# A two-layer graph network: layer 1's attention weights carry both exponentials, its fetched rows go to the matmul as they are, and TensorE counts the used columns

## The chip, the cores and the metric

One core of one Trainium2 chip runs the whole program. The metric is the device time of one execution in microseconds (us); lower is better. Engines are called PE (TensorE), DVE (VectorE), ACT (ScalarE), POOL (GpSimd) and SP (SyncE, which only issues DMAs here).

## The reference, cut to what matters

There are 16 graphs of N = 1024 nodes with F = 256 features. Layer 0 is a graph attention with batch normalisation; the change leaves its code alone. Layer 1 has H = 4 heads and is where the change lies:

```
fts = inputs @ Wh                      # inputs: layer 0's result after residual and layernorm
f1, f2 = fts @ w1h + b1h, fts @ w2h + b2h
coefs_logits = softmax(leaky_relu(f1[:, None] + f2[None, :], 0.2) - 1e9 * (1 - adj))
coefs = ah * coefs_logits + (1 - ah) * softmax(adj)
vals = coefs @ fts + bh
head = elu(vals + inputs)              # mean of the four heads, residual, layernorm
```

The adjacency is sparse: an edge from i to j has a probability that falls with both indices. In a block of 128 target rows, most columns have no edge at all. The kernel therefore finds, for each block of rows, the columns that are used, fetches only these columns' rows of the table, and sums over them.

## The kernel before, in words

N is cut into K = 8 blocks of P = 128 rows. For block q at most CAPS[q] × 128 used columns are fetched, with CAPS = (6, 4, 3, 3, 3, 3, 2, 2): 26 fetches of 128 columns per graph, numbered c. For each c there is `xc[c]`, 128 rows of a table `xe_dram` (256 features, a one, four values of a first exponential and four of a second), and `mc[c]`, the same columns' 128 mask values for the block's rows (bf16). `A[it]` holds an exponential of f1 for the rows of block `it`, for four heads, spread over all partitions.

The softmax of a leaky ReLU is split so that no exponential is taken per edge. For head h the weight of an edge is max(A, exp(-0.8 f2)) times the mask, made by DVE (`Unit.weights`, L1356, one 128x128 operation per column block and head, 1664 in all). The other factor, exp(f2), is multiplied into the fetched row by ACT (`Unit.values`, L1347, 128x257, also 1664). PE multiplies the two (`gather`, L1378) and gets the sum over edges and, in column 257, the divisor.

Work is laid out in **units**: one unit is one block of rows and two heads (`hp`), 16 units per graph, 256 in all. Nothing here is left to a scheduler: the body stands in `tc.manual_schedule()`, and each engine works its instructions in the order in which the loop issues them. One pass n of the loop handles six units at different stages: `add` (n-3, DVE), `turned` (n-2, ACT), `addends` (n, POOL), `gather` (n, PE), `linear` (n-2, PE), `mix` (n-1, DVE) and `turn` (n-1, PE), weights and values for n+2, `exps` (n-3, ACT), `share` (n, ACT), `sum` (n-3, DVE), `close` (n-4). Every second unit has the heavy `sum`, which ends with layernorm statistics and, on POOL, a power of -0.5 (`inv_std`, L159).

After this each pass issues the **side steps** of the next graph, by a table from pass number to steps (`side`): load of h, mask and x, `elu`, `used` (which columns have an edge), `places` (prefix counts by matmul), `pick` (eight one-hot tiles `oh` by DVE, L1134, with matmuls that turn them into index lists), `residual` (transpose of h by PE, then add and layernorm statistics by DVE), `norm`, `factors`, `spread`, `scale`, `table`, `split`, `total`, `neighbours` (the sum over all neighbours by PE, then one addition by DVE, L1293) and the fetches. A graph's fetches begin in pass 11 of the graph ahead of it.

PSUM tiles of the side steps come from one pool of two buffers, `ps_s`. Three queues issue DMAs: SP (loads, stores and the transposed mask load L1061), POOL (indirect fetches and `mask`, L1278, which turns a block of the mask into fp32), and ACT (layer 0 alone).

In these terms `used` works on the transposed mask in SBUF, `mt`: it takes a maximum over the 128 rows of each block by halving (L1082, L1087) and one reduction (L1091).

Of the kernel before, what the change touches and what calls it, by code (L numbers as in the profile page):

```python
# [8 lines left out]
F32 = mybir.dt.float32  # L9
# [10 lines left out]
P = 128  # L20
# [7 lines left out]
def kernel(  # L28
# [93 lines left out]
    iota16 = cpool.tile([P, P], FP16, name="iota16")  # L122
# [6 lines left out]
    with tc.tile_pool(name="ipool", bufs=1) as ipool:  # L129
        ii = ipool.tile([P, P], I32, name="ii")  # L130
        nc.gpsimd.iota(ii, pattern=[[1, P]], base=0, channel_multiplier=0)
# [905 lines left out]
    with ExitStack() as l1:  # L1037
# [8 lines left out]
        class Graph:  # L1046


            def __init__(self, b):
                self.b = b  # L1050
                self.S, self.mr, self.xc, self.mc, self.A = {}, {}, {}, {}, {}

            def load_h(self):
                b = self.b
                self.h = hpool.tile([P, C, N], F32, tag="h", name=f"h_{b}")
                nc.sync.dma_start(self.h, h_dram[b])
                if b in ready1:
                    self.mt = ready1[b]
                else:
                    self.mt = m1pool.tile([P, K, N], BF16, tag="mt", name=f"mt1_{b}")  # L1060
                    nc.sync.dma_start_transpose(self.mt, adj16[b])  # L1061
                self.mv = pk.tile([P, K, 2], F32, tag="mv", name=f"mv_{b}", bufs=2)
# [7 lines left out]

            def used(self):

                b = self.b
                nc.sync.dma_start(
                    mt_dram[b % 2][0:N, :].rearrange("(k p) i -> p k i", p=P), self.mt
                )
                self.act = pk.tile([P, K, K], BF16, tag="act", name=f"act_{b}", bufs=2)
                for half in range(2):
                    ks = slice(half * K // 2, (half + 1) * K // 2)
                    view = self.mt[:, ks, :].rearrange("p k (q i) -> p k q i", i=P)  # L1080
                    t = pk.tile([P, K // 2, K, P // 2], BF16, tag="hm", name=f"un_{b}_{half}", bufs=1)
                    nc.vector.tensor_tensor(  # L1082
                        t, view[:, :, :, 0 : P // 2], view[:, :, :, P // 2 : P], ALU.max
                    )
                    n = P // 4
                    while n >= 8:
                        nc.vector.tensor_tensor(  # L1087
                            t[:, :, :, 0:n], t[:, :, :, 0:n], t[:, :, :, n : 2 * n], ALU.max
                        )
                        n //= 2  # L1090
                    nc.vector.tensor_reduce(self.act[:, ks, :], t[:, :, :, 0 : 2 * n], AX.X, ALU.max)  # L1091

            def places(self):


                b = self.b
                pp = ps_s.tile([P, K + 1, K], F32, tag="s", name=f"pp_{b}")
                for k in range(K + 1):
# [5 lines left out]
                    if k < K:  # L1104
                        nc.tensor.matmul(pp[:, k, :], tri16, self.act[:, k, :], start=(k == 0), stop=False)
                        nc.tensor.matmul(pp[:, k, :], far16, self.act[:, k, :], start=False, stop=True)
                pos = pk.tile([P, K + 1, K], F32, tag="pos", name=f"pos_{b}", bufs=1)
                nc.scalar.copy(pos, pp)
# [5 lines left out]
                nc.vector.tensor_copy(self.r16, pi)  # L1114
                nc.vector.tensor_tensor(pos[:, 0:K, :], pos[:, 0:K, :], self.r16, ALU.subtract)
# [6 lines left out]
                self.t16 = pk.tile([P, K, K * n], FP16, tag="t16", name=f"t16_{b}", bufs=2)  # L1122
# [3 lines left out]
                )  # L1126

            def pick(self, q):

                b = self.b  # L1130
                if q == 0:
                    self.pl = ps_s.tile([P, NC], F32, tag="s", name=f"pl_{b}")
                oh = pk.tile([P, K, P], FP16, tag="oh", name=f"oh_{b}_{q}", bufs=2)
                nc.vector.tensor_tensor(  # L1134
                    oh, iota16.unsqueeze(1).to_broadcast([P, K, P]),
                    self.r16[:, :, q : q + 1].to_broadcast([P, K, P]), ALU.is_equal,
                )
                n = max(CAPS)
                for k in range(K):
                    nc.tensor.matmul(  # L1140
                        self.pl[:, CAT[q] : CAT[q] + CAPS[q]],
                        oh[:, k, :], self.t16[:, k, q * n : q * n + CAPS[q]],
                        start=(k == 0), stop=(k == K - 1),
                    )
# [9 lines left out]
            def fetch_rows(self, c):  # L1154

                self.xc[c] = pk.tile([P, XW], F32, tag="xc", name=f"xc_{self.b}_{c}", bufs=14)
# [5 lines left out]
            def fetch_mask(self, c):  # L1162

                self.mc[c] = pk.tile([P, P], BF16, tag="mc", name=f"mc_{self.b}_{c}", bufs=14)
# [6 lines left out]
            def rows(self, it):  # L1171
# [3 lines left out]
                    self.A[it], a_dram[self.b][:, it * P : (it + 1) * P].partition_broadcast(P)  # L1175
                )
# [13 lines left out]
            def residual(self, k):  # L1190
                nm = f"{self.b}_{k}"
                pz = ps_s.tile([P, F], F32, tag="s", name=f"pz_{nm}")
                for oc in range(C):
                    nc.tensor.transpose(
                        pz[:, oc * P : (oc + 1) * P], self.h[:, oc, k * P : (k + 1) * P], ident
                    )
                xk = self.x[:, k, 0:F]
# [432 lines left out]
```

## Time and profile before

| | |
|---|---|
| time, median of 3 runs | 3520.68 us (3514.99 to 3521.13) |
| the profiled execution: its own time | 3522.07 us |
| its span in the profile | 3520.3 us |
| granted TensorE clock, mean | 0.859 |
| busy: PE, DVE, ACT, POOL | 77%, 80%, 55%, 43% of the span |
| layer 0, up to about | 798 us |
| layer 1, first graph's preparation, up to the first weights | 883 us |
| layer 1, one graph in the steady part (first `o` to first `o`) | 168.2 us |

The page cuts the span into 40 slices of 88 us, a digit for the busy tenths of each engine. In its list of costly groups a row gives the source line, engine and operation, output and inputs, shape and count, then busy time in all and the mean duration of one, then the engine's idle time just before these instructions and what ended most of it. Durations of neighbouring instructions on one engine overlap, so the distance from start to start is the price where an engine works without a break.

### The profile page before, as it was taken

The numbers are of one execution on the slowest core, as the hardware profiler recorded it, in microseconds if no ns is written. First come the engines' busy times: TensorE is split into PE (matmuls) and PEld (weight loads), VectorE is DVE, ScalarE is ACT, GpSimd is POOL, SyncE is SP. The second block draws the span as 40 slices with busy tenths as digits, with TensorE's granted clock in tenths as the row PEclk, the third lists the DMA queues.
The fourth block names the chain that finished last, engine by engine and source line by source line (L and its number), as shares of the span: only waits on it lengthen the run. The fifth ranks groups of instructions, "written<-read, shape, count | busy, mean of one in ns | idle before, by whom it ended". The sixth has DMA issues, their size and how long they took to land.

```text
span 3520.3 us, 44899 instructions
## 1 busy us (share of the span) xinstructions
PE 2722.9 (77%) x14567; PEld 2126.6 (60%) x14567; DVE 2804.3 (80%) x6644; ACT 1919.1 (55%) x3892; POOL 1510.7 (43%) x1425
## 2 busy tenths in 40 slices
PE   7936999994786877777777768686868686867796
PEld 6723444443675756566665657575757575756575
DVE  3369999974888787888878787878787878787888
ACT  1247777751564655555555555555556464645565
POOL 0000000003564646455646465555646464646463
PEclk9957999996897978788888888888889797978898
DMA  9796985555464747464646455554546464737441
GB/s 279 220 260 151 234 212 154 152 154 116 99 125 99 136 102 139 90 142 80 143 91 145 86 133 102 127 104 115 108 113 124 105 124 97 141 92 147 90 89 40
DMA packets 630643, 462.90 MB, mean 131 GB/s; under 512 B 286424, under 2 KB 567040, under 8 KB 624256
## 3 DMA queue, kind: packets, MB, share of 16 engines
q1 hardware_dynamic: 446016, 286.63, 30.3%
q0 software_dynamic: 183168, 170.81, 28.5%
q8 instruction: 118, 1.93, 0.2%
q10 hardware_dynamic: 1216, 2.51, 0.2%
q14 instruction: 125, 1.02, 0.1%
HBM read 257.53 MB, written 135.21 MB: 112 GB/s over the span
## 4 chain that ended last, share of the span: by engine, by line
DVE 37%; PE 26%; issue 16%; DMA 9%; ACT 6%; POOL 5%; SPq 0%; DVEq 0%; ACTq 0%; POOLq 0%
DVE w L1356 8%; PE pu L1378 7%; DMA mt<-adj 6%; PE pm L1288 4%; PE pa L584 4%; PE pw L301 4%; PE pv L1418 3%; DVE s L1398 3%; DVE v L1425 2%; DVE oh L1134 2%; DVE xs L1257 2%; POOL xc L1157 2%; PE pf L1208 2%; ACT x L1224 2%; DVE z L1396 2%
## 5 line engine op out<-in xcount | busy, mean ns | idle before, releaser
L1378 PE MATMUL pu<-g,w 128*128 128x257 f32 x3328 | 944.2, 444 | 3.1 <-ACT g L1347 3.1
L1378 PEld LDWEIGHTS pu<-g,w 128*128 128x128 f32 x3328 | 740.3, 230 | 128.9 <-ACT g L1347 3.6
L1347 ACT ACTIVATE g<-xc 128x257 f32<-128x257 f32 x1664 | 723.0, 502 | 65.5 <-DMA xc<-xe_dram,ix 55.2
L1418 PE MATMUL pv<-W1s,sT 128*128 128x256 f32 x2048 | 524.8, 402 | 269.9 <-DVE z L1394 257.2
L1418 PEld LDWEIGHTS pv<-W1s,sT 128*128 128x128 f32 x2048 | 400.3, 200 | 371.5 <-issue 267.1
L1356 DVE SCALAR_TENSOR_TENSOR w<-A,xc,mc 128x128 f32<-128x128 f32 x1664 | 586.1, 420 | 37.9 <-DMA xc<-xe_dram,ix 30.7
L1157 POOL DMA_INDIRECT xc<-xe_dram,ix x416 | 480.9, 1156 | 144.0 <-issue 121.0
L1165 POOL DMA_INDIRECT mc<-mt_dram,im x416 | 443.6, 1066 | 130.0 <-issue 110.3
L584 PE MATMUL pa<-em,wh 128*128 128x512 f32 x1024 | 451.8, 599 | 17.9 <-issue 13.4
L159 POOL TENSOR_TENSOR ors<-ors,mhalf 128x1 f32<-128x1 f32 x128 | 98.0, 766 | 788.3 <-DVE ors L158 674.1
L1429 ACT ACTIVATE m<-v,neg 128x512 f32<-128x512 f32 x256 | 183.3, 716 | 443.7 <-DVE z L1394 242.7
L1288 PE MATMUL pm<-xs,mr 128*128 128x256 f32 (+1 forms) x2048 | 292.4, 302 | 75.1 <-DMA mr<-mt 75.1
L584 PEld LDWEIGHTS pa<-em,wh 128*128 128x128 f32 x1024 | 193.7, 192 | 251.0 <-issue 236.3
L1288 PEld LDWEIGHTS pm<-xs,mr 128*128 128x128 f32 x2048 | 274.5, 206 | 78.1 <-issue 78.1
L1366 POOL TENSOR_TENSOR v<-x,bias 128x512 f32<-128x512 f32 x256 | 311.9, 1218 | 22.7 <-DVE acc L1436 13.5
L1398 DVE SCALAR_TENSOR_TENSOR s<-pu,z,s 128x256 f32<-128x256 f32 x512 | 224.3, 480 | 24.5 <-ACT s L1388 0.5
L1388 ACT ACTIVATE s<-S,q 128x256 f32<-128x256 f32 x512 | 228.9, 495 | 0.0
L1412 ACT COPY sT<-pt 128x512 f32<-128x512 f32 x256 | 148.1, 578 | 94.1 <-PE pt L1406 86.2
L540 ACT ACTIVATE e<-eb,c,s 128x1024 f32<-128x1024 f32 x128 | 155.0, 1236 | 79.1 <-DVE sm L554 42.7
L1457 ACT ACTIVATE o<-o,ors 128x256 f32<-128x256 f32 x128 | 76.8, 600 | 204.8 <-DVE ors L1454 196.3
L1293 DVE SCALAR_TENSOR_TENSOR S<-pm,X 128x256 f32<-128x256 f32 x128 | 54.0, 423 | 158.3 <-PE pm L1288 138.5
L1425 DVE TENSOR_TENSOR v<-pv,v 128x512 f32<-128x512 f32 x256 | 173.6, 678 | 0.5 <-PE pv L1418 0.5
(256 smaller groups left out, 3921.9 us busy)
## 6 DMA issues: line engine op xcount, KB each, us to landing
mr<-mt POOLq DMA_DIRECT2D x128, 512.0 KB
x<-in_x_dram SPq DMA_DIRECT2D x32, 1024.0 KB
adj<-in_adj_dram POOLq DMA_DIRECT2D x16, 2048.0 KB
mt_dram<-mt SPq DMA_DIRECT2D x16, 2048.0 KB
A<-a_dram SPq DMA_DIRECT2D x128, 256.0 KB
xe_dram<-x SPq DMA_DIRECT2D x16, 1060.0 KB
wh_dram<-wx SPq DMA_DIRECT2D x16, 1024.0 KB
wh<-wh_dram SPq DMA_DIRECT2D x16, 1024.0 KB
```

What stands on the lines that cost most here:

```text
L584: nc.tensor.matmul(acc[b, hf, oc], wh[b][:, k, oc * P : (oc + 1) * P], ems[b, k][:, hf * HALF : (hf + 1) * HALF], start=(k == 0), stop=(k ...
L1157: nc.gpsimd.indirect_dma_start(out=self.xc[c], out_offset=None, in_=xe_dram[self.b % 2], in_offset=bass.IndirectOffsetOnAxis(ap=self.ix[:, ...
L1165: nc.gpsimd.indirect_dma_start(out=self.mc[c], out_offset=None, in_=mt_dram[self.b % 2].rearrange("n (q i) -> (n q) i", i=P), in_offset=ba ...
L1288: nc.tensor.matmul(pm[:, 0:n], lhsT, self.xs[:, k, part, 0:n], start=(k == 0 and part == 0), stop=(k == K - 1 and part == 0),)
L1347: nc.scalar.mul(v, g.xc[c][:, 0:F1], g.xc[c][:, F1 + H + h : F1 + H + h + 1])
L1356: nc.vector.scalar_tensor_tensor(w, g.A[self.it][:, h, :], g.xc[c][:, F1 + h : F1 + h + 1], g.mc[c], ALU.max, ALU.mult,)
L1366: nc.gpsimd.tensor_tensor(self.v2, self.g.x[:, self.it, 0:F].unsqueeze(1).to_broadcast([P, HP, F]), bias1[:, h : h + HP, :], ALU.add,)
L1378: nc.tensor.matmul(self.pu[:, hh, 0:F1], self.w[hh][t], self.v[hh][t], start=(t == 0), stop=(t == n - 1),)
L1388: nc.scalar.mul(self.s[:, hh], g.S[it], g.q[:, it, h0 + hh : h0 + hh + 1])
L1398: nc.vector.scalar_tensor_tensor(s[:, hh], self.pu[:, hh, 0:F], z[:, hh : hh + 1], s[:, hh], ALU.mult, ALU.add)
L1418: nc.tensor.matmul(self.pv[:, hh, :], self.sT[:, hh, fc, :], W1s[:, fc, self.hp * HP + hh, :], start=(fc == 0), stop=(fc == C - 1),)
L1425: nc.vector.tensor_tensor(self.v2, self.pv, self.v2, ALU.add)
```

## The change

**Weights.** The table's exponentials become exp(f2) and exp(0.2 f2). With A = exp(0.8 f1) the weight max(A · exp(f2), exp(0.2 f2)) is the softmax's numerator up to a factor of the row. It is made per column block c for four heads: four `tensor_scalar` (multiply, maximum, both with a pointer operand) and one product with the mask over 128x512. ACT's scaled copies of the rows fall away: `gather` takes `xc[c]` as the moving side. A column block's weights serve both units of a block.

**Used columns.** A graph's adjacency rows are loaded once more, untransposed, as `rw` (2 MB, bf16). PE counts each block's edges per column by 64 matmuls with one column of ones; DVE takes the minimum with 1. The one-hot tile `oh` lies in `rw`'s buffer and has the block index innermost, so that every operand has unit steps.

**Residual.** One `tensor_tensor_reduce` adds and sums the row; the square sums are ACT's (`means`, eight Square activations with accumulator), in place of bn_stats and bn_aggr.

**Order.** A side step's matmuls and its DVE part are issued apart: `first` goes ahead of `mix` and `turn`, `after` to the end of the pass. The power of -0.5 of `sum` is issued a pass later (`power`), `close` at n-5. Weights are made three passes ahead, fetches start one pass earlier; mask and `rw` are loaded in pass 14 of the graph two ahead. Buffers: xc and mc 17 (14), w 12 of four heads, m 1, s 2.

```diff
-    iota16 = cpool.tile([P, P], FP16, name="iota16")
+    iota16 = cpool.tile([P, P, K], FP16, name="iota16")
...
+            def load_mask(self):
...
+                self.rw = pk.tile([P, K, N], BF16, tag="rw", name=f"rw_{b}", bufs=1)
+                nc.sync.dma_start(self.rw, adj16[b].rearrange("(q p) j -> p q j", p=P))
...
+            def counts(self):
+                self.pc = ps_s.tile([P, K, K], F32, tag="s", name=f"pc_{self.b}")
+                for k in range(K):
+                    for q in range(K):
+                        nc.tensor.matmul(
+                            self.pc[:, k, q : q + 1], self.rw[:, q, k * P : (k + 1) * P],
+                            ones16[:, 0:1], start=True, stop=True,
+                        )
             def used(self):
-                for half in range(2):
-                    ...
-                    nc.vector.tensor_reduce(self.act[:, ks, :], t[:, :, :, 0 : 2 * n], AX.X, ALU.max)
+                nc.vector.tensor_scalar(self.act, self.pc, 1.0, None, ALU.min)
...
+            def mark(self, q):
                 nc.vector.tensor_tensor(
-                    oh, iota16.unsqueeze(1).to_broadcast([P, K, P]),
-                    self.r16[:, :, q : q + 1].to_broadcast([P, K, P]), ALU.is_equal,
+                    self.oh[:, q], iota16, self.r16[:, q, :].unsqueeze(1).to_broadcast([P, P, K]),
+                    ALU.is_equal,
                 )
...
+            def weights(self, c):
+                it = max(q for q in range(K) if CAT[q] <= c)
+                w = self.w[c] = pk.tile([P, H, P], F32, tag="w", name=f"w_{self.b}_{c}", bufs=12)
+                xc = self.xc[c]
+                for h in range(H):
+                    nc.vector.tensor_scalar(
+                        w[:, h, :], self.A[it][:, h, :], xc[:, F1 + h : F1 + h + 1],
+                        xc[:, F1 + H + h : F1 + H + h + 1], ALU.mult, ALU.max,
+                    )
+                nc.vector.tensor_tensor(
+                    w, w, self.mc[c].unsqueeze(1).to_broadcast([P, H, P]), ALU.mult
+                )
...
             def residual(self, k):
-                nc.vector.tensor_tensor(xk, pz, xk, ALU.add)
-                nc.vector.bn_stats(st, xk)
-                nc.vector.bn_aggr(self.mv[:, k, :], st)
+                nc.vector.tensor_tensor_reduce(
+                    out=xk, in0=self.pz[k], in1=xk, scale=1.0, scalar=0.0,
+                    op0=ALU.add, op1=ALU.add, accum_out=self.mv[:, 0, k : k + 1],
+                )
...
+            def means(self):
+                nc.vector.tensor_scalar(self.mv[:, 0], self.mv[:, 0], -1.0 / F, None, ALU.mult)
+                for k in range(K):
+                    d = pk.tile([P, F], BF16, tag="d", name=f"d_{self.b}_{k}", bufs=2)
+                    nc.scalar.activation(
+                        d, self.x[:, k, 0:F], AF.Square, bias=self.mv[:, 0, k : k + 1], scale=1.0,
+                        accum_out=self.mv[:, 1, k : k + 1],
+                    )
...
-            def values(self, hh):
-                    ...
-                    nc.scalar.mul(v, g.xc[c][:, 0:F1], g.xc[c][:, F1 + H + h : F1 + H + h + 1])
-            def weights(self, hh):
-                    ...
-                    nc.vector.scalar_tensor_tensor(
-                        w, g.A[self.it][:, h, :], g.xc[c][:, F1 + h : F1 + h + 1], g.mc[c],
-                        ALU.max, ALU.mult,
-                    )
...
                     nc.tensor.matmul(
-                        self.pu[:, hh, 0:F1], self.w[hh][t], self.v[hh][t],
+                        self.pu[:, hh, 0:F1], g.w[c][:, h, :], g.xc[c][:, 0:F1],
...
+            after[-2] += [g.load_mask]
+            after[-1] += [g.load_h]
+            first[2] += [g.counts]
+            after[2] += [g.used, each(g.elu, 0)]
+            first[3] += [g.places]
+            after[3] += [g.load_x, g.placed, each(g.elu, 1)]
+            for k in range(K):
+                first[4 + k // 2] += [each(g.turn, k)]
+                after[4 + k // 2] += [each(g.residual, k)]
+            after[5] += [g.store_mask]
+            for q in range(K):
+                after[4 + q // 3] += [each(g.mark, q)]
+            after[7] += [g.means, g.norm]
+            first[8] += [g.pick, g.shares1]
+            after[8] += [g.indices, g.factors]
+            ...
+            for it, n in enumerate((11, 12, 12, 13, 13, 14, 14, 15)):
+                first[n] += [each(g.neighbours, it)]
+                after[n] += [each(g.summed, it)]
+            for it, n in enumerate((6, 7, 8, 11, 12, 12, 13, 13)):
+                after[n] += [each(g.mask, it)]
...
+            for n in range(len(units) + 6):
+                b, i = divmod(n, NU)
+                do(n - 3, "add")
+                do(n - 2, "turned")
+                do(n - 4, "power")
+                do(n, "addends")
+                if n < len(units):
+                    units[n].gather(0)
+                    units[n].gather(1)
+                do(n - 2, "linear")
+                stand(0, b, i)
+                do(n - 1, "mix", "turn")
+                for s, at in ((b + 1, i), (b, NU + i)):
+                    if s < B:
+                        made(graphs[s], at)
+                do(n - 3, "exps")
+                do(n, "share")
+                do(n - 3, "sum")
+                do(n - 5, "close")
+                stand(1, b, i)
```

`stand(0, …)` issues a pass's `first` steps and `stand(1, …)` its `after` steps, for the graph one ahead, for the one two ahead and for the graph at hand.

## The prediction

> **What bounds the kernel now.** The profile page comes first: engine totals, then the slices.
>
> ```profile
> PE 2722.9 (77%) x14567; PEld 2126.6 (60%) x14567; DVE 2804.3 (80%) x6644; ACT 1919.1 (55%) x3892; POOL 1510.7 (43%) x1425
> ...
> DVE  3369999974888787888878787878787878787888
> ```
>
> No engine is full. From slice 10 on (about 880 us) the picture repeats sixteen times: layer 1, one graph of 16 units at a time, while the side steps of the next graph are worked in. The first `o` of each graph comes 168.2 us after the one before (mean of 14 periods in the trace). To see where a period goes I cut one (graph 5) at each `v<-pv` of L1425, the first DVE step of a loop pass, and asked for busy times by stretch. Passes i = 0, 1, 4, 7, 11 and 14:
>
> ```profile
> core 0: us, PE busy (x) PEld busy (x) DVE busy (x) ACT busy (x) POOL busy (x), PEclk, DMA share, GB/s
> 1715.46:1724.31 8.85, 8.85 (x43) 7.30 (x41) 8.46 (x24) 7.77 (x18) 3.20 (x3) 1.00 0.62 168
> 1724.31:1743.08 18.77, 5.89 (x29) 4.87 (x28) 15.17 (x28) 7.77 (x14) 9.48 (x9) 0.82 1.09 267
> ...
> 1762.85:1775.77 12.92, 8.77 (x65) 7.18 (x66) 12.07 (x27) 4.51 (x10) 6.56 (x5) 0.76 0.25 76
> ...
> 1797.90:1806.37 8.47, 7.76 (x52) 7.22 (x50) 5.03 (x20) 3.32 (x7) 4.02 (x4) 0.89 0.36 62
> ...
> 1836.92:1845.53 8.61, 8.61 (x58) 8.03 (x57) 5.53 (x15) 4.42 (x11) 5.31 (x6) 1.00 0.66 111
> ...
> 1860.94:1874.38 13.44, 10.87 (x59) 9.65 (x57) 11.11 (x34) 8.52 (x22) 11.39 (x12) 0.87 0.69 111
> ```
>
> A pass lasts about as long as the busier of PE and DVE in it, and then some: summed over the 16 passes (mean of 13 graphs) the larger of the two is 152 us, the period 168. The other 16 us are waits, and the query of waits (1200 to 3200 us, 12 graphs) names them (us in total, times, longest):
>
> ```profile
> DVE S L1293 <- PE pm L1288: 88.5, 62, 3.5
> DVE h L1188 <- ACT h L1185: 36.9, 12, 3.1
> DVE x L1198 <- PE pz L1194: 27.6, 11, 3.2
> ...
> DVE f L1232 <- PE pf L1208: 23.6, 12, 2.6
> ...
> PE pv L1418 <- DVE z L1394: 207.8, 67, 15.5
> PE pl L1140 <- DVE oh L1134: 104.1, 96, 3.0
> ```
>
> A side step's matmuls stand on PE behind `turn`, so behind DVE's `mix`; DVE then waits for them at once. Two queues take turns where both have work. The period is DVE work, PE work in some passes, and this ping-pong. ACT (91.7 us a period) has slack.
>
> [...] nine L446 `tensor_scalar` of 1024 take 6.05 us (662 ns apart), while `oh`, 16 bit but with a step-0 inner operand, takes 1135 ns for 1024 and `un`, 2048 bf16, 1225. [...] of 847 `w` that run beside a POOL DMA_INDIRECT alone 3 exceed 400 ns, of 116 that meet a POOL TENSOR_TENSOR 93 do (up to 2119). [...] 16 small `r` casts, 195 ns each. [...] Here `pu` matmuls stand 217 or 425 ns apart, nothing between.
>
> ```profile
> 1700.50 1.93 DVE L1356 SCALAR_TENSOR_TENSOR w<-A,xc,mc 128x128 f32<-128x128 f32 x7 [0.89 <-DMA xc<-xe_dram,ix]
> 809.20 9.16 DVE L1134 TENSOR_TENSOR oh<-iota,r 128x1024 f16<-128x1024 f16 x8
> L1347 ACT ACTIVATE g<-xc 128x257 f32<-128x257 f32 x1664 | 723.0, 502 | 65.5 <-DMA xc<-xe_dram,ix 55.2
> L1356 DVE SCALAR_TENSOR_TENSOR w<-A,xc,mc 128x128 f32<-128x128 f32 x1664 | 586.1, 420 | 37.9 <-DMA xc<-xe_dram,ix 30.7
> ```
>
> Durations overlap, so I price by start to start: `w` 262 ns (7 in 1.93 us).
>
> **Part by part, us per graph (one period).** DVE:
> - Weights: 104 `w` at 0.262 = 27.2 go. In come 104 `tensor_scalar` of 128 with pointers: [...] 0.196, 20.4 in all; and 26 products of 128x512: 0.60 (spacing of L1436) + 0.08 behind their own last input (L1439 stands 0.12 further off) = 17.7. **+10.9**. [...]
> - `used`: L1082, L1087, L1091 (2.5 + 2.8 + 0.8) become one small operation: **-6.0**.
> - `oh`: 8 × 1.135 = 9.1 becomes 8 × 0.60 with unit steps: **-4.3** (0 if not).
> - Residual: add, bn_stats, bn_aggr (3.2 + 3.4 + 0.8) become 8 adds with an accumulator, 0.35 + 0.08 (L189 shows 346 apart with its read): 3.4 or so: **-4.0**.
> - Small new ones: +0.3. DVE total **-3**.
>
> ACT: 104 `g` (42.8) go, 8 Square with accumulator come: 128x256 is about 0.5, read 0.19 (L606): 5.5. **-37**, hidden but where DVE waits for ACT. PE: `gather` has the same shapes; +64 one-column matmuls at 26 ns (`pl` is 27) = **+1.7**; `pick` reads weights with a step of 8 elements, which no row shows: 0 to 64 × 0.1 = 6, I take 0. POOL: same operations; 8 `pow` are one pass later, so fetches no longer queue behind a `pow` that waits for DVE. Fetches and weights start a pass earlier. SP: 2 MB `rw` more per graph, behind the transpose that holds SP 14.6 us; four passes of cover (38 us), DMA share is about 0.55. If that cover goes, `counts` and PE behind it wait.
>
> Order is the large part: side matmuls now stand ahead of `mix`, their DVE halves at the end of the pass. The S, x and f waits and `pl`'s go (7.4 + 2.3 + 2.0 on DVE, 8.7 on PE). New: in pass 7 `means` sends 8 Squares to ACT and `norm`, next on DVE, waits for them: 5.5, then POOL's `pow` 1.7 and latencies: **+7.5** against 1.8 now; behind it on DVE stands the next `add`, for which PE's `linear` waits. `elu` keeps its ACT wait once (2.9).
>
> What is late next at `neighbours` is the mask: masks 4 to 6 are issued in the pass before their use, and PE waits 4.0 a period for such DMAs today (47.8 over 12).
>
> Passes rebuilt: DVE = 5.2 (even i: heavy `sum`) or 2.75 (odd) + 1.4 per column made (2, 2, 1, 2, 1, 2, 1, 2, 1, 1, 1, 1, 1, 3, 3, 2) + side: `elu` 1.4 in passes 2 and 3, `placed` 2.1 in 3, residuals and marks 2.7, 2.7, 2.1 in 4 to 6, `norm` 1.3, `factors` 1.6, `split` 1.7 and 1.6, `summed` 0.4 to 0.8, `shares` 1.2. PE = gather (per column and pass four `pu`, 0.24 each) + `linear` and `turn` 2.35 + side (`counts` 1.7; `pl` and `pf` 5.3 in pass 8; `pX` and `pm` 3.7 in 11, then `pm` 1.9 each), clock about 0.9. Larger of the two plus the waits named and some POOL blocking, i = 0 to 15: 8.3, 8, 11.5, 9.6, 9.9, 8.8, 9.2, 14.3, 10.5, 7.5, 8.7, 9, 8, 8.4, 10.8, 7.7 = 150. Pass 1 falls most (18.8 to 8: `elu` and `used` leave it), pass 7 grows. Of the kernel before, a rebuild by busy times missed 16; here most waits are counted, and I add 4: **154**, so -14 × 15 graphs = **-210**.
>
> The start: graph 0's `rw` and the h and x loads behind it must wait for layer 0's memory, issued near 799; 2 MB at the 200 GB/s of neighbouring slices is 10 us, where `used` took 7: +5. The fetches: 20 (mask and row of two blocks) at 1.25 stand ahead of mask 3, where 13 stood: +9. **+15** (5 to 20). End: close is a pass later, ACT lighter: -2 to +2, 0. Sum: 3522.07 (the profiled execution; span 3520.3 plus 1.8; 1.4 above the median) - 210 + 15 = 3327, less 1.4: **3325**.
>
> **Rivals.**
> 1. Passes overlap more than the larger-of-two rule: DVE 125 + POOL blocking 8 + pass 7's and other waits 10 = 143: 3520 - 25 × 15 + 15 = **3160**. For: PE's gather may run a pass ahead. Against: passes before never beat their busier engine.
> 2. It doesn't do what it says: [...] +11.2 × 15 = 168: **3493**. [...]
> 3. Slower: [...] (0.96 us, L1157's median): 26 × 0.96 = 25 a period, +375: **3700**. It decides from (3520 - 3325)/15/26 = 0.50 us a column. For: POOL prepares DMAs over a third of the time. Against: the casts above, and a preparation can stretch instead (up to 4.3 us beside `oh`), which costs only fetch slack.
>
> **How the numbers follow.** Likeliest case 0.52 (own range 3250 to 3400), rival 1 0.20, rival 2 and kin (waits left over) 0.15, rival 3 0.11, no change 0.02. Faster by over 0.2% (about what a measurement can tell) 0.87, within 0.02, slower 0.11. The range leaves out rival 3 and the low half of rival 1: 3170 to 3490.
>
> **What would show it.** After: period near 154; `w` products and `tensor_scalar` near 200 ns apart; `oh` 0.6; pass 1 about 8 us, pass 7 about 14 with DVE waiting for ACT's Square; no S <- pm or pl <- oh. Wrong if `tensor_scalar` lasts over 0.6 us beside POOL, or PE waits for `rw`.

## The result: 3602.93 us, slower by 2.4%

| | before | after |
|---|---|---|
| median, same chip (4 runs each) | 3517.84 us | 3602.93 us |
| ratio, 95% interval | | 1.0243 (1.0225 to 1.0261) |
| span of the profiled execution | 3520.3 us | 3601.0 us |
| first `o` of graph 0 | 940.2 us | 962.2 us |
| steady part: mean of the 16 passes' sum, 13 graphs | 168.2 us | 172.1 us |

The 81 us of span are: start +22, fourteen periods +54 (+3.9 each), the step from graph 14 to 15 +10.8, the last graph -8.2, the end +1.9. The prediction had -14 a period and +15 at the start.

Engine totals and DVE's slices of the page after:

```profile
PE 2810.2 (78%) x15591; PEld 2233.4 (62%) x15591; DVE 2777.1 (77%) x6820; ACT 1319.3 (37%) x2484; POOL 1392.6 (39%) x1425
...
DVE  4369999953877878787878787868787877878788
```

ACT lost 600 us of work and DVE 27, PE gained 87; only PE is fuller, by one percent of the span, and the program is slower. So the time has to be looked for in single passes. These are the same graph's passes i = 0, 1, 4, 7, 8, 9, 11, 14, cut at the same DVE step as before (columns as there: length, busy time of PE, weight loads, DVE, ACT, POOL, then the granted clock):

```profile
core 0: us, PE busy (x) PEld busy (x) DVE busy (x) ACT busy (x) POOL busy (x), PEclk, DMA share, GB/s
1754.25:1762.90 8.65, 8.65 (x44) 7.60 (x43) 8.27 (x25) 1.52 (x3) 3.00 (x4) 1.00 1.12 261
1762.90:1775.13 12.23, 7.86 (x39) 6.56 (x37) 6.84 (x19) 3.08 (x6) 3.74 (x4) 0.95 0.66 240
1796.76:1807.13 10.37, 7.13 (x28) 5.67 (x28) 10.03 (x27) 2.59 (x5) 4.76 (x5) 0.84 0.28 89
1826.05:1839.52 13.47, 5.44 (x28) 4.55 (x28) 7.27 (x27) 6.03 (x20) 1.78 (x2) 0.84 0.07 16
1839.52:1855.43 15.91, 15.08 (x108) 14.23 (x109) 9.25 (x25) 2.12 (x4) 10.76 (x11) 0.50 0.67 107
1855.43:1866.79 11.36, 9.79 (x39) 7.62 (x37) 6.54 (x20) 8.27 (x21) 2.22 (x2) 0.83 0.39 110
1876.87:1886.43 9.56, 8.74 (x45) 8.02 (x46) 4.69 (x15) 1.79 (x4) 0.08 (x1) 0.67 0.20 22
1906.84:1919.56 12.72, 8.00 (x52) 7.24 (x52) 12.23 (x33) 2.71 (x7) 9.46 (x10) 1.00 0.75 122
```

The eye should stop at three lines. Pass 1 lasts 12.2 us with no engine over 7.9: a wait. Pass 8 lasts 15.9 with PE at 15.1 and a clock of 0.50. Pass 9 lasts 11.4 with PE 9.8 and ACT 8.3, neither full: two engines taking turns. Against the prediction, as means over 13 graphs:

| pass | 0 | 1 | 2 | 3 | 4 | 5 | 6 | 7 | 8 | 9 | 10 | 11 | 12 | 13 | 14 | 15 |
|---|---|---|---|---|---|---|---|---|---|---|---|---|---|---|---|---|
| before | 8.8 | 19.7 | 9.9 | 9.9 | 12.9 | 11.1 | 10.7 | 9.9 | 11.3 | 9.4 | 9.8 | 8.6 | 6.7 | 7.6 | 14.8 | 7.2 |
| predicted | 8.3 | 8 | 11.5 | 9.6 | 9.9 | 8.8 | 9.2 | 14.3 | 10.5 | 7.5 | 8.7 | 9 | 8 | 8.4 | 10.8 | 7.7 |
| after | 8.7 | 11.0 | 11.6 | 10.0 | 10.4 | 9.1 | 9.8 | 13.5 | 15.9 | 11.4 | 10.1 | 9.2 | 9.8 | 10.0 | 12.9 | 8.8 |

Passes 8, 9 and 1 make 12 of the 22 us above the predicted 150; passes 10 and 12 to 15 make 8. The query of waits (same window of 2000 us, total us, times, longest) names what stands in the first three:

```profile
PE pv L1429 <- DVE z L1405: 333.1, 92, 8.0
...
DVE acc L1447 <- ACT m L1440: 92.3, 22, 4.8
...
ACT X L1308 <- PE pX L1303: 85.1, 11, 8.5
DVE f L1264 <- PE pf L1231: 66.8, 11, 6.1
...
DVE w L1192 <- DMA A<-a_dram: 47.3, 12, 5.1
DVE mv L1249 <- ACT d L1241: 45.2, 11, 4.1
```

The old waits for `pz` and `pl` are gone, as predicted, and of 88.5 us for `pm` 3.9 are left (24.5 more at the same addition, in pass 12, are listed with the releaser `remote`). In their place DVE waits for ACT's exponentials (passes 9 and 11), for `pf` (pass 8), for A (pass 1) and for the Squares (pass 7). Passes 7 and 8 as the timeline has them (start, duration, and in brackets the idle time before with its releaser):

```profile
1837.29 0.17 DVE L1249 TENSOR_SCALAR mv<-mv 128x8 f32<-128x8 f32 x1 [4.11 <-ACT d L1241]
...
1837.74 1.66 POOL L159 TENSOR_TENSOR rs<-rs,mhalf 128x8 f32<-128x8 f32 x1 [12.76 <-DVE rs L158]
...
1839.43 0.17 DVE L1251 TENSOR_TENSOR rs<-mv,rs 128x8 f32<-128x8 f32 x1 [1.77 <-POOL rs L159]
...
1840.35 3.75 PE L1429 MATMUL pv<-W1s,sT 128*128 128x256 f32 x8 [8.03 <-DVE z L1405]
...
1843.89 3.99 PE L1143 MATMUL pl<-t,oh 128*128 128x6 f16 x64
...
1847.74 6.98 PE L1231 MATMUL pf<-WW,h 128*128 128x8 f32 x32
...
1854.76 0.22 DVE L1264 TENSOR_TENSOR f<-pf,xw 128x64 f32<-128x64 f32 x1 [6.09 <-PE pf L1231]
```

DVE stands 4.1 + 1.8 us in `norm`, as forecast. PE therefore stands 8 us, and then works 15 us at a granted clock of 0.50: `pv` 426 ns apart in place of 216, `pf` 213 in place of 112. And `pl` lasts 3.99 us for 64, 60 ns each, where before it was 27.

The weights, and `oh`, at full speed (timeline; the last figure is the count in the group, its time the whole group's):

```profile
815.26 4.90 DVE L1132 TENSOR_TENSOR oh<-iota,r 128x1024 f16<-128x1024 f16 x8
...
1211.73 1.12 DVE L1192 TENSOR_SCALAR w<-A,xc 128x128 f32<-128x128 f32 x4
1212.89 0.69 DVE L1196 TENSOR_TENSOR w<-w,mc 128x512 f32<-128x512 f32 x1
```

`oh` came out as priced: 8 in 4.90 us, 602 ns apart. The product too: 609. A `tensor_scalar` is 256 ns from the next, not 196. In the steady part (13 graphs, cut as above) DVE is busy 50.6 us a graph with weights, against 36.2 before.

### The profile page after: what moved, and what is told of

Same layout as the page of the kernel before. It is cut to its first block, busy times and chain, and to the rows that moved or that the text cites. A ratio compares the mean times of both kernels' runs of the same rounds, so it can differ in the third digit from the quotient of the medians.

```text
span 3601.0 us, 45794 instructions
## 1 busy us (share of the span) xinstructions
PE 2810.2 (78%) x15591; PEld 2233.4 (62%) x15591; DVE 2777.1 (77%) x6820; ACT 1319.3 (37%) x2484; POOL 1392.6 (39%) x1425
## 4 chain that ended last, share of the span: by engine, by line
DVE 32%; PE 12%; issue 9%; DMA 9%; POOL 6%; ACT 6%; SPq 2%; another core or an unknown queue 1%; DVEq 0%; POOLq 0%; ACTq 0%
DVE w L1192 8%; PE pv L1429 4%; DMA A<-a_dram 4%; DVE w L1196 3%; PE pf L1231 3%; DVE v L1436 3%; DMA mc<-mt_dram,im 2%; DVE s L1409 2%; DVE xs L1293 2%; POOL v L1376 2%; ACT d L1241 2%; POOL mc L1173 2%; PE pl L1143 2%; DVE v L1449 2%; DMA mr<-mt 2%
## 5 line engine op out<-in xcount | busy, mean ns | idle before, releaser
L1429 PE MATMUL pv<-W1s,sT 128*128 128x256 f32 x2048 | 659.2, 479 | 566.9 <-DVE z L1405 432.8
L1429 PEld LDWEIGHTS pv<-W1s,sT 128*128 128x128 f32 x2048 | 469.1, 238 | 716.7 <-issue 478.5
L1389 PE MATMUL pu<-xc,w 128*128 128x257 f32 x3328 | 821.2, 400 | 11.3 <-DVE w L1196 9.1
L1389 PEld LDWEIGHTS pu<-xc,w 128*128 128x128 f32 x3328 | 656.6, 204 | 104.9 <-DVE w L1196 12.2
L1192 DVE TENSOR_SCALAR w<-A,xc 128x128 f32<-128x128 f32 x1664 | 508.3, 376 | 54.0 <-DMA A<-a_dram 54.0
L1165 POOL DMA_INDIRECT xc<-xe_dram,ix x416 | 417.9, 1005 | 144.0 <-issue 123.8
L1173 POOL DMA_INDIRECT mc<-mt_dram,im x416 | 426.0, 1024 | 104.9 <-issue 100.1
L1196 DVE TENSOR_TENSOR w<-w,mc 128x512 f32<-128x512 f32 x416 | 317.0, 762 | 14.2
L1463 POOL TENSOR_TENSOR ors<-ors,mhalf 128x1 f32<-128x1 f32 x128 | 72.8, 569 | 300.3 <-DVE ors L1469 284.6
L1314 POOL DMA_DIRECT2D mr<-mt x128 | 121.0, 947 | 166.2 <-PE pm L1324 139.7
L1447 DVE SCALAR_TENSOR_TENSOR acc<-m,v 128x512 f32<-128x512 f32 x128 | 87.8, 686 | 125.9 <-ACT m L1440 125.9
```

The costliest lines, as they stand in the source:

```text
L1165: nc.gpsimd.indirect_dma_start(out=self.xc[c], out_offset=None, in_=xe_dram[self.b % 2], in_offset=bass.IndirectOffsetOnAxis(ap=self.ix[:, ...
L1173: nc.gpsimd.indirect_dma_start(out=self.mc[c], out_offset=None, in_=mt_dram[self.b % 2].rearrange("n (q i) -> (n q) i", i=P), in_offset=ba ...
L1192: nc.vector.tensor_scalar(w[:, h, :], self.A[it][:, h, :], xc[:, F1 + h : F1 + h + 1], xc[:, F1 + H + h : F1 + H + h + 1], ALU.mult, ALU.max,)
L1196: nc.vector.tensor_tensor(w, w, self.mc[c].unsqueeze(1).to_broadcast([P, H, P]), ALU.mult)
L1389: nc.tensor.matmul(self.pu[:, hh, 0:F1], g.w[c][:, h, :], g.xc[c][:, 0:F1], start=(c == cs[0]), stop=(c == cs[-1]),)
L1429: nc.tensor.matmul(self.pv[:, hh, :], self.sT[:, hh, fc, :], W1s[:, fc, self.hp * HP + hh, :], start=(fc == 0), stop=(fc == C - 1),)
```

## Experiments

Two theories stood at first. **A**: the weights took work from ACT, which had slack, and gave it to DVE, the busiest engine before the change. **B**: the new order brought new waits, and these hold the period whatever DVE does. Every time below is a ratio to the kernel before on the same chip, beside the sum of the 16 passes.

### The weights alone, and everything but the weights

`b_weights` is the kernel before with this part only, its buffers included (in short):

```diff
-    weights: 4 x scalar_tensor_tensor(max, mult) per column; values: ACT, xc times exp(f2)
+    weights: 4 x tensor_scalar(mult, max) and one 128x512 product per column, shared by two units
-    nc.tensor.matmul(self.pu[:, hh, 0:F1], self.w[hh][t], self.v[hh][t], ...)
+    nc.tensor.matmul(self.pu[:, hh, 0:F1], g.w[c][:, h, :], g.xc[c][:, 0:F1], ...)
```

> The kernel before with the weights part alone: four tensor_scalar and one product of 128x512 per column block, shared by both units of a block, ACT's scaled rows gone, gather takes the fetched rows; everything else (order, used columns, one-hot tiles, residual) as before; xc and mc 17 buffers, w 12. DVE gains about 15 us a graph, ACT loses 43. Theory A: slower than the kernel before, 168 -> 176 to 184 a graph, ratio 1.04 to 1.08, more than the whole change costs, so that the rest of the change is worth -5 to -12 a graph. Rival B (the loss comes from the new order and its waits, the weights are about neutral because passes were held by waits and ACT's relief pays back): ratio 0.98 to 1.01.

`a_split` is the changed kernel with this part's arithmetic undone:

```diff
-    nc.vector.tensor_scalar(w[:, h, :], A, xc[F1 + h], xc[F1 + H + h], ALU.mult, ALU.max)   # 4 heads
-    nc.vector.tensor_tensor(w, w, mc, ALU.mult)
+    nc.vector.scalar_tensor_tensor(w[:, h, :], A, xc[F1 + h], mc, ALU.max, ALU.mult)       # 4 heads
...
+    nc.scalar.mul(w[:, h, :], w[:, h, :], xc[F1 + H + h])                                   # after exps
```

> The changed kernel with the weights alone put back to the old arithmetic: per column block and head one DVE operation (maximum with exp(-0.8 f2), then times the mask), and ACT multiplies exp(f2) into the weight (128x128, in place, after exps). Order, counts, residual and buffers stay as changed. DVE loses 104 x 0.256 + 26 x 0.61 - 104 x 0.262 = 15 us a graph, ACT gains 104 x 0.3 to 0.4 = 31 to 42. Theory A (the weights moved work from an ACT with slack onto DVE, which bounds most passes): the passes with DVE on top shorten, about -0.6 a column, 172 -> 157 to 162 a graph, total 3350 to 3440, ratio to the kernel before 0.95 to 0.98. Rival B (the period is held by the waits of passes 1, 7, 8 and 9 and by the order, whatever DVE does): 169 to 174 a graph, ratio 1.01 to 1.03. Rival C (ACT with 90 us a graph delays exps and sT): slower than the changed kernel.

| order, counts, residual | old weights | new weights |
|---|---|---|
| as before | 1 (168.2) | 1.0497, 1.0470 to 1.0523 (178.0) |
| as changed | 0.9804, 0.9776 to 0.9832 (163.3) | 1.0243, 1.0225 to 1.0261 (172.1) |

Theory A holds for the weights part as a whole, in both orders; that DVE's time is the reason is shown by `a_ts512` below, where ACT is untouched. The new weights cost 9.8 us a graph in the old order and 8.8 in the new; everything else in the change gains 5 to 6. DVE's line of the two pages says how:

```profile
PE 2779.7 (75%) x14567; PEld 2146.8 (58%) x14567; DVE 3111.0 (84%) x7060; ACT 1259.4 (34%) x2228; POOL 1455.2 (39%) x1425
```

```profile
PE 2760.2 (80%) x15591; PEld 2188.7 (63%) x15591; DVE 2479.9 (72%) x6404; ACT 1819.5 (53%) x4148; POOL 1451.1 (42%) x1425
```

The first is `b_weights`, the second `a_split`. With the weights alone DVE is busy 156.2 us a graph in place of 137.1 (+19.1), and 9.8 of it reach the period; with them undone it is busy 116.9 in place of 135.4 (-18.5), and 8.8 do. About half of a DVE microsecond reaches the end. `a_split`'s ACT multiplies a 128x128 weight and not a 128x257 row, so this cell of the table is not the old scheme to the letter. Rival C, that a busy ACT would delay `exps` and lose the gain, fell.

### What a tensor_scalar costs

`a_tsmix` gives the operations of the four heads different operands. Where an operand is a column of `xc` (a pointer), each partition has its own value; where it is a number, all have the same:

```diff
+    tensor_scalar(w[:, 0], A[:, 0], e1[0:1], e2[0:1], mult, max)
+    tensor_scalar(w[:, 1], A[:, 1], e1[1:2], 0.0,     mult, max)
+    tensor_scalar(w[:, 2], A[:, 2], 1.0,     0.0,     mult, max)
+    tensor_scalar(w[:, 3], A[:, 3], e1[3:4], e2[3:4], mult, max)
```

> The changed kernel with four different tensor_scalar of 128x128 per column block: head 0 with two pointer operands, head 1 with a pointer and an immediate, head 2 with two immediates, head 3 with two pointers (heads 1 and 2 leave their own factors out). It prices the operation. 341 ns at 128 and 540 at 512 wide are 0.52 ns an element[...]; yet two stand 256 ns apart[...]. Theory (each pointer operand has its own fixed cost): 256, about 226, about 196 ns to the next. Rival (256 ns is the fixed cost of any 128-wide tensor_scalar behind another): all three near 256.

One column block of `a_tsmix` in the timeline:

```profile
1867.13 0.34 DVE L1192 TENSOR_SCALAR w<-A,xc 128x128 f32<-128x128 f32 x1
1867.38 0.28 DVE L1193 TENSOR_SCALAR w<-A,xc 128x128 f32<-128x128 f32 x1
1867.58 0.22 DVE L1194 TENSOR_SCALAR w<-A 128x128 f32<-128x128 f32 x1
1867.71 0.34 DVE L1195 TENSOR_SCALAR w<-A,xc 128x128 f32<-128x128 f32 x1
```

Read the differences of the starts: two pointers 0.25, one 0.20, none 0.13. Over all 416 blocks the medians are 254, 196 and 135 ns: **each pointer operand costs 60 ns**, in spacing and in duration (341, 282, 222). At the 0.52 ns an element of the next run, 128 elements are 67 of the 135 ns, and 68 are left as fixed, an estimate from these two runs. The old `w`, with one pointer, fits the same sum at 1.04 ns an element (worked out below): 133, 68 and 60 are 261, measured 262. The kernel took 3562.63 us in a single run, with 169.6 us a graph: 2.5 of the 4.7 us that DVE saves (26 times 60 and 120 ns).

`a_ts512` makes one instruction of the four, and leaves out the own factors of heads 1 to 3:

```diff
-    for h in range(H): nc.vector.tensor_scalar(w[:, h, :], self.A[it][:, h, :], ...)
+    nc.vector.tensor_scalar(w, self.A[it], xc[:, F1 : F1 + 1], xc[:, F1 + H : F1 + H + 1], ...)
```

> The changed kernel with one tensor_scalar of 128x512 per column block, with head 0's two pointers, in place of four of 128x128: the other heads' own factors are left out. ACT, PE, POOL, order and DMAs are untouched. At the 256 ns of a 128-wide one, the wide one tells the slope: [...] DVE loses 104 x 0.256 - 26 x (0.40 to 0.66) = 9.5 to 16 us a graph. Theory A (DVE bounds most passes): the period falls by 60 to 90% of that, 172 -> 158 to 166, ratio 0.96 to 0.995. Rival B (waits hold it): under 3 us a graph, ratio 1.01 to 1.02.

540 ns at 512 wide against 341 at 128 is 0.52 ns an element, half of the 1.04 that an fp32 `scalar_tensor_tensor` takes in the kernel before (687 ns at 512, 1218 at 1024). So by the element a `tensor_scalar` with two pointers **is** the faster of the two. (The 574 ns to the next instruction includes the product's wait for its own input.) Ratio 0.9913 (0.9884 to 0.9942), 164.7 a graph: DVE lost 14.4, the period 7.4. Again about half, with ACT, PE and all DMAs untouched. That is the cleanest evidence for theory A; of the expected 60 to 90% only 51 came, because the wait for A grew from 47 to 82 us in the window and ate a part.

### The waits one by one

**A of block 2.** On SP's queue this load stands behind the next graph's transposed mask load, issued in pass 14 (11.0 us of SP in one such pass).

```diff
-    after[NU - 5 + 2 * it] += [each(g.rows, it)]
+    after[NU - 5 + 2 * it - (2 if it == 2 else 0)] += [each(g.rows, it)]
```

> The changed kernel with the load of A for block 2 issued in pass 13 in place of 15, so that on SP's queue it stands ahead of the next graph's transposed mask load of pass 14. Theory (the weights of pass 1 wait 3.9 us a graph for this load, behind the transpose): pass 1 goes from 11.0 to about 8 us, -2 to -3.9 a graph, ratio 1.005 to 1.015. Rival (the wait hides a wait for the fetched rows or the mask, which comes next): under 1 us.

Ratio 1.0100 (1.0063 to 1.0137), 168.4 a graph. Pass 1 went from 11.0 to 7.0 us, and no wait for A is left:

```profile
DVE acc L1447 <- ACT m L1440: 92.9, 23, 4.6
DVE f L1264 <- PE pf L1231: 73.2, 12, 6.1
DVE mv L1249 <- ACT d L1241: 49.3, 12, 4.1
```

The first three of its waits are the other three of the list above; nothing came in A's place.

**The pause, the clock and `pick`.** Four kernels: the Squares spread out (`a_means`), PE kept at work in its pause (`a_warm`), `pf` ahead of `pl` (`a_swap`), `pick`'s weights without a step (`a_ohk`).

```diff
 a_means
-    after[7] += [g.means, g.norm]
+    after[4 + j] += [g.means(2 * j, 2 * j + 1)]      # j = 0..3, behind their residuals
+    after[7] += [g.norm]
 a_warm
+    for _ in range(96): nc.tensor.matmul(pw[:, 0:128], ones16, far16, ...)   # pass 8, before linear
 a_swap
-    first[8] += [g.pick, g.shares1]
+    first[8] += [g.shares1, g.pick]
 a_ohk
-    self.oh = pk.tile([P, K, P, K], ...);  matmul(..., self.oh[:, q, :, k], ...)
+    self.oh = pk.tile([P, K, K, P], ...);  matmul(..., self.oh[:, q, k, :], ...)
```

> The changed kernel with the eight Squares of means issued two at a time at the end of passes 4 to 7, right behind the residuals of their blocks, in place of all eight in pass 7; norm stays in pass 7. Clock theory (PE idles 8 us in pass 7 because DVE waits for the Squares, and the clock granted in pass 8 is 0.50 for that reason, so that pick and shares1 run at half speed): pass 7 loses 4 us and pass 8 another 4 to 6, -8 to -10 a graph, ratio 0.98 to 0.99. Rival, stall only (the 0.50 comes from the small matmuls of pass 8 themselves): -3 to -4 a graph, ratio 1.005 to 1.012. Third (the Squares' time comes back in passes 4 to 6 and 7 is held by POOL's power): under 2 us a graph, ratio 1.015 to 1.025.

Ratio 1.0056 (1.0037 to 1.0075), 167.5 a graph: pass 7 lost 2.9, pass 8 lost 1.7. By its size this is the rival's, by its place it has something of both: the pause shrank and pass 8 with it, but `pf` was still 208 ns apart on average.

> The changed kernel with 96 extra 128x128 bf16 matmuls on PE in pass 8, behind gather and ahead of linear, which nobody reads (they stand where PE waits 8 us for DVE's mix of pass 7). [...] Clock theory: PE does not cool down, the granted clock in pass 8 goes from 0.50 to 0.9 or 1.0, pf from 213 to about 110 ns and pl from 60 to about 30 ns apart, pass 8 from 15.9 to 11 us, -3 to -5 a graph, ratio 1.00 to 1.007. Rival (pl's strided weights and pf's narrow output are slow by their shape): pl stays near 60 ns and pass 8 stays at 15 to 16, ratio 1.02 to 1.03.

Ratio 1.0128 (1.0101 to 1.0154), 169.4. Pass 8 lost 2.0 us, less than the clock theory asked, and the clock by stretches of 2 us shows why (after the five busy times comes PEclk):

```profile
1826.72:1828.72 2.00, 2.00 (x22) 1.76 (x20) 1.90 (x8) 1.28 (x3) 1.69 (x2) 1.00 0.78 104
1828.72:1830.72 2.00, 2.00 (x28) 1.88 (x27) 1.97 (x6) 0.24 (x1) 1.67 (x3) 1.00 1.35 179
1830.72:1832.72 2.00, 2.00 (x37) 2.00 (x36) 1.97 (x3) 0.00 (x0) 1.70 (x3) 1.00 0.25 68
1832.72:1834.72 2.00, 2.00 (x18) 2.00 (x17) 1.90 (x4) 0.00 (x0) 1.69 (x2) 0.63 2.10 279
1834.72:1836.72 2.00, 2.00 (x11) 2.00 (x11) 0.62 (x6) 0.60 (x1) 1.80 (x3) 0.50 0.27 68
```

The 96 extra matmuls took 5.52 us, 57 ns each. The pass begins at 1.00 and `linear` takes 1.97 us in place of 3.75. `pl` begins at 1829.35. Four us later, with PE counted as busy throughout, the clock falls to 0.50, and `pf`, which begins at 1833.18, pays: it stays at 0.50 for all of its 6.9 us. Two things are told apart here: `pl`'s 60 ns are the same at either clock, and the clock falls behind `pl` without any pause. The rival was right on the first, the clock theory on the start of the pass.

> The changed kernel with pass 8's two groups of side matmuls in the other order: pf (32, fp32) ahead of pl (64, fp16, strided weights). With dummy matmuls in PE's pause the clock of pass 8 began at 1.00 and fell to 0.63 and 0.50 four us after pl began, and pf again took 213 ns each; pl was 60 ns apart at either clock. Theory (pl's short matmuls do not hold the clock up, and pf pays for standing behind them): pf's first ten or so run at 213 and the rest at 112 ns, pass 8 from 15.9 to about 13.5, -2 to -3 a graph, ratio 1.008 to 1.015. Rival (the pause alone sets the clock for the whole pass): pf stays at 213 ns, under 1 us. Against both: factors comes earlier by pl's 3.9 us but indices waits longer; they stand together at the end of the pass.

Ratio 1.0183 (1.0154 to 1.0213), 170.7; pass 8 lost 1.0. From one graph's timeline, and its clock in stretches of 2 us:

```profile
1835.37 3.75 PE L1429 MATMUL pv<-W1s,sT 128*128 128x256 f32 x8 [6.36 <-DVE z L1405]
1838.91 4.05 PE L1231 MATMUL pf<-WW,h 128*128 128x8 f32 x32
1842.81 3.99 PE L1143 MATMUL pl<-t,oh 128*128 128x6 f16 x64
...
1838.54:1840.54 2.00, 2.00 (x14) 1.91 (x12) 1.97 (x3) 0.00 (x0) 1.70 (x3) 0.69 0.27 68
1840.54:1842.54 2.00, 2.00 (x20) 2.00 (x19) 1.86 (x5) 0.00 (x0) 1.69 (x2) 1.00 2.15 286
1842.54:1844.54 2.00, 2.00 (x33) 2.00 (x33) 0.64 (x4) 0.60 (x1) 1.46 (x3) 0.66 0.27 69
```

In front, `pf` takes 4.05 us here in place of 6.98. The clock went from 0.50 to 1.00 at 1839.8 (an estimate from the mean of 0.69 in the first stretch), 4.4 us after `linear` began. But the mean of 0.66 in the third stretch puts its fall at 1843.2 in the same way: 4.3 us after `pf` began, when `pl` had run for 0.4 us. So here the clock fell behind `pf`, with 8 moving columns, as it fell four us into `pl` in `a_warm`. And the rise comes in time for `pf` in 6 of the 13 graphs only, where pass 8 lasts 13.0 to 14.3 us; in the other seven `pf` is as slow as before and the pass lasts 15.9. That is why the mean gained 1.0 and not 2.9.

> The changed kernel with the one-hot tile laid the old way (block index ahead of the column, so that pick's weights are read without a step, and DVE's compare has a step-0 operand again). Theory (pl's 60 ns are the step of 8 elements between weights): pl 25 to 30 ns apart, pick 2 us shorter, oh from 602 to about 1135 ns, DVE +4.3 us in passes 4 to 6. Those passes have DVE on top (9.7 of 10.4), so +2 to +4 there and -2 in pass 8: 171 to 174 a graph, ratio 1.02 to 1.035. Rival (pl's 60 ns come from standing alone without other matmuls between): pl stays near 60 ns and the ratio is 1.03 to 1.045.

`pl` fell from 60 to 26 ns: the step was the cause, at 34 ns a matmul, 2.2 us in 64. Why a step costs this is not shown. But the ratio was 1.0526 (1.0485 to 1.0567), worse than both theories had it: in my version the index operand kept a step of 8 elements beside the step-0 one, and `oh` took 1856 ns and not 1135. Passes 4 to 6 grew by 3.7, 3.7 and 2.4 us, 10 for 10 us of DVE, so in those passes DVE's time comes through whole. Pass 8 lost 3.0.

**ACT's copies.** Pass 9 on ACT in the changed kernel:

```profile
1855.93 4.03 ACT L1256 ACTIVATE x<-x,rs 128x256 f32<-128x256 f32 x8
1859.86 0.57 ACT L1423 COPY sT<-pt 128x512 f32<-128x512 f32 x1
1862.62 0.25 ACT L1360 COPY ar<-pA 32x128 f32<-32x128 f32 x1 [2.19 <-PE pA L1358]
1862.79 0.72 ACT L1440 ACTIVATE m<-v,neg 128x512 f32<-128x512 f32 x1
```

Eight `scale` hold up `sT`, for which PE's `linear` waits; `spread` stands behind `linear` on PE, the copy `ar` waits 2.2 us for it, and `m` is behind `ar`. The copies were moved:

```diff
-    (spread, total, in `first`)  nc.scalar.copy(ar, pb);   nc.scalar.copy(self.X, px)
+    (own steps, in `after`)      nc.scalar.copy(ar, self.pb);   nc.scalar.copy(self.X, self.px)
```

> The changed kernel with ACT's two copies of side results out of PSUM (ar in pass 9, X in pass 11) moved from ahead of the pass's exps to the end of the pass; PE's part stays where it was. In the changed kernel they wait for PE on ACT's queue (X 7 us, ar 2 us a graph), exps stand behind them, and DVE's acc or v behind exps (92 us of waits for m over 11 graphs). Theory (this wait is on the path): passes 9 and 11 lose 1 to 4 us each, -3 to -6 a graph, ratio 0.995 to 1.01. Rival (the wait only comes to DVE where PE holds the pass anyway, pass 11 being PE's): under 1.5 us a graph, ratio 1.018 to 1.025.

Ratio 1.0177 (1.0147 to 1.0207), 170.7: -1.4 a graph, by size the rival's. The wait for `m` fell from 92 to 20 us in the window and pass 9 from 11.4 to 9.1; 0.7 came back in pass 10, and pass 11 did not move (9.2 to 9.1): there DVE waits 51 us in the window for `pm` now. So the theory was right for pass 9 and the rival for pass 11.

### Together

`a_all` is `a_rows2`, `a_means`, `a_swap` and `a_xcopy` in one, with graph 0's mask fetches ahead of its preparation again; `a_allsplit` adds `a_split`.

> The changed kernel with four reordered steps together: Squares spread over passes 4 to 7, A of block 2 loaded in pass 13, ACT's X and ar copies at the end of their passes, pf ahead of pl in pass 8; and for graph 0 the mask fetches of the first two blocks issued ahead of the preparation again, as in the kernel before (only the row fetches wait for the table). New weights stay. Alone the four gave -4.6, -3.7, -1.4 and -1.4 us a graph. Theory (separate waits in separate passes, they add): 172 -> 160 to 162, first o 8 to 12 us earlier than 962, total 3415 to 3445, ratio 0.970 to 0.980. Rival (each wait hides the next): 165 or more, ratio 0.985 or more.

> The same four reordered steps and the same start, with the weights put back to the old arithmetic (one DVE operation per head, ACT multiplies exp(f2) into the weight after exps). With the waits in place, putting the weights back gave -8.8 us a graph of the 15 to 18 that DVE lost. Theory (waits gone, DVE is more often the bound, so that more of the weights' DVE time comes through): -10 to -15 against the same steps with new weights, a period of 147 to 152, total 3230 to 3300, ratio 0.92 to 0.94. Rival (the same half, or less, as PE takes over): -5 to -9, 152 to 157, ratio 0.94 to 0.96.

| | ratio, 95% interval | median | us a graph |
|---|---|---|---|
| `a_all` | 0.9797 (0.9753 to 0.9840) | 3443.57 | 162.0 |
| `a_allsplit` | 0.9265 (0.9237 to 0.9293) | 3263.53 | 150.5 |

The four waits add: 10.1 of the 11.1 us that they gave singly. With them gone the weights' 18.8 us of DVE are worth 11.5 a graph, 61% in place of 48. Not all passes gained: pass 13 grew from 10.0 to 13.0 us in `a_all`, where PE waits 3.6 us a graph for a mask block, the lateness that the prediction named at `neighbours` (window of 2000 us, 12 times):

```profile
PE pm L1331 <- DMA mr<-mt: 42.7, 12, 4.1
```

`a_allsplit` is faster than both kernels, by 7.3% against the one before. Its totals, and its passes 1 and 8:

```profile
PE 2709.2 (83%) x15591; PEld 2161.9 (66%) x15591; DVE 2469.9 (76%) x6449; ACT 1821.7 (56%) x4148; POOL 1456.6 (45%) x1425
```

```profile
1652.21:1657.81 5.60, 5.60 (x29) 4.83 (x29) 5.42 (x17) 4.01 (x11) 3.75 (x4) 1.00 1.06 392
...
1715.84:1730.80 14.96, 14.13 (x109) 13.69 (x110) 7.73 (x25) 3.40 (x8) 10.96 (x11) 0.56 0.72 114
```

Pass 1, 19.7 us in the kernel before, is now as long as PE's work in it. Pass 8 is still PE, at a clock of 0.56 in this graph, and with a mean of 13.5 us the largest piece left; in 5 of the 13 graphs `pf` finds the full clock and the pass lasts 11.

## Why the prediction was wrong

**Right:** `used` and the residual (an add with its accumulator read is 0.43 us from the next, so 3.4 for eight, as forecast, against 7.4 for the three operations), `oh`'s 0.60 and the product's 0.60 + 0.08 (measured 602 and 609), the end of the x and `pl` waits and of most of S, pass 7 (predicted 14.3, measured 13.5, with the 4.1 for Squares and 1.8 for POOL's power that were named), and that PE does not wait for the `rw` load in the steady part. Rival 3, weights that wait out a DMA preparation on POOL (0.96 us), did not happen: 98 of 1664 `tensor_scalar` lasted over 450 ns, and 93 of the 1664 old ones did.

**The weights' term, +10.9.** It took 196 ns for a `tensor_scalar`, my estimate from L446 (662 ns for 1024), whose operands the step did not look at: L446 has one pointer and the number 0.5, and 196 ns is what one pointer costs in `a_tsmix`. Two pointers make it 256: 6.2 us a graph more. So it costs nearly what an old `w` did, 256 against 262 ns: of the 66 ns that 128 elements at 0.52 and not 1.04 ns save, the second pointer takes 60. In the old order the term was 18.1 (36.2 to 54.3), in the new one 14.4. Yet DVE's total was nearly right, -1.7 against -3, and this error alone, at half its size, is 3 of the 18 us by which the period was missed.

**"Larger of the two plus the waits named".** This step failed most, for passes 8, 9 and 1. Redone on the trace, the larger of PE and DVE summed over the passes is 152.4 us a graph (152.6 before), which alone is more than the 150 forecast with waits; another 19.7 us are waits, against 15.6 before.
- Pass 8 (+5.4): PE was costed with "clock about 0.9" and `pick`'s step "I take 0". The pass 7 stall was in the sum, but not the clock of 0.50 with which PE leaves it: `linear` +1.8. Nor was it asked what clock is granted behind matmuls with 2 to 8 moving columns (0.50 in the changed kernel): `pf` +3.2 (32 at 213 and not 112), with or without the stall (`a_warm`). The step of the weights adds 2.2 in `pl`. The bound of 0 to 6 for it held; the value chosen, 0, was too low, and the clock had no bound.
- Pass 9 (+3.9): ACT's -37 was called "hidden but where DVE waits for ACT", and where that is was not asked. `scale` stands ahead of `turned` and `ar` ahead of `exps`; the run with the copies moved took 2.2 of it.
- Pass 1 (+3.0): fetches and weights a pass earlier were costed at nothing. SP's queue was named for `rw` and not for A, which now stands behind the transpose. The run with A earlier took 4.0.
- Passes 10 and 12 to 15 (+8 together) were not taken up singly. Undoing the weights shortens 13, 14 and 15 by 2.0, 2.9 and 1.6, so a good part is DVE's weights (3, 3 and 2 columns are made there); pass 12 stays at 9.7. DVE waits 2.1 us a graph in it for what the list calls `remote`, and the cause stays open.

**The start, +15:** it was 22. The fetches are the +9 forecast (mask 3 was issued at 864.4 and is at 872.7): with their old place restored as well, `a_all` has its first `o` at 954.5, where the four other steps, each alone, leave it at 963. DVE waited 11.6 us for the counts of `rw`, where the old `used` took 6.4. The new weights cost time here too, which the forecast left out of the start: in `b_weights`, where the preparation is the old one, the first `o` comes at 951.5, 11 us later than before, and undoing them in the new order (`a_split`) takes back 5. What the wait for `rw` adds was not taken apart.

**The rivals.** None had the mechanism. Rival 2 (weights and `oh` without the gain forecast for them, and its kin, waits left over) came nearest in kind; its 3493 still gave the new order all that the forecast gave it. The rival for slower put all its weight on POOL's DMA preparation, so the chance of slower, 0.11, was the chance of the wrong cause. "ACT's slack" was in the first paragraph of the prediction: work that leaves an engine with slack for one without is the plainest rival, and it wasn't drawn up.

## What to carry to other kernels

Before counting a smaller instruction total as a gain, ask for each engine whether it had slack in the passes where work is added or taken; here no run shows a gain from the 600 us taken from ACT (the same half of DVE's change came through with ACT relieved and with ACT untouched), and of each us laid on DVE half came through over the period (in passes 4 to 6 of `a_ohk` all of it). A stall can have a second price on PE: here, after one of 8 us, the granted clock was 0.50 (`linear` 426 ns apart in place of 216), and it stayed there through the 11 us of matmuls with 2 to 8 moving columns that followed. When a step moves earlier, go down every queue that it is moved on, loads included, and write what it stands behind.

## What the runs showed that was not expected

- Pointer operands of `tensor_scalar` cost 60 ns each: 135, 196 and 254 ns apart with none, one and two, at 128 fp32 elements.
- Four us after matmuls with 2 to 6 moving columns (`pl`, in `a_warm`) began, the granted clock fell from 1.00 to 0.50, though PE shows as busy for all of that time; in `a_swap` it fell 4.3 us after those with 8 (`pf`) began. What the two share is the small number of columns; no run varies it alone.
- With fp16 weights read at a step of 8 elements a matmul takes 60 ns, at either clock, in place of 26.
